# GpSimd's instructions in the order of the kernel's own clock, and a longer margin for ScalarE's steps in the tridiagonal form

## The chip, the cores and the metric

One core of a Trainium2 chip runs the whole program. The time is that of one execution on the device, in microseconds; for the kernel before it is the median of three runs. Engines are named as in the profile: PE is TensorE's matmul, PEld its weight load, DVE is VectorE, ACT is ScalarE, POOL is GpSimd, SP is SyncE.

## What is computed

64 graphs `x` of 256 nodes by 256 features, one matrix `adj` of 256 by 256. Two layers, each `x = x + f(relu(layernorm(x)))`.

```python
# layer 0, w = adj * adj
h = relu(w @ (h @ W1)); h = relu(w @ (h @ W2)); f = w @ (h @ W3)      # 256 -> 512 -> 1024 -> 256 features
# layer 1
deg = adj.sum(0) + adj.sum(1) - diag(adj)
L = rsqrt(deg)[:, None] * (diag(deg) - A) * rsqrt(deg)[None, :]      # A: adj
_, U = eigh(L)
f = U @ (relu((U.T @ h) @ W1 + b1) @ W2 + b2)                        # 256 -> 128 -> 256 features
```

The eigenvectors `U` of one symmetric 256 by 256 matrix are needed before layer 1 can begin; layer 0 doesn't need them.

## The kernel before

Two pieces of work run side by side until the eigenvectors are there.

The **chain** is the eigenvector computation of class `Eigen`: the Laplacian, its tridiagonal form (`tridiagonalize`, 254 steps of Householder's reduction), an iteration on leaves of 16, and four levels of merging. Its steps depend on each other one by one, and most of them run on VectorE.

The **streams** are layer 0 of class `Layers`, over 32 pairs of graphs (`products` and `rows`): large products on TensorE, evictions and norms on ScalarE, and on GpSimd two kinds of work. One is the norm's three operations, `v`, `scale` (a power) and `shift`, named so in the profile. The other is three accumulating transfers a pair, `forms<-forms`, `s<-s` and `s<-forms`.

Class `Pace` interleaves them while the program is written out. It keeps a clock for each engine and the time at which each piece of a tile is written or was read. Every operation of the chain goes through `chain`: its due time is the time at which its operands are ready, plus `LATER` (0.4 us on PE, 0.1 on ACT). Before it is issued, `run` issues operations of the streams, earliest first, as long as `fits` allows: on PE and ACT they have to begin or end before the due time, by the engine of the chain's operation; on every other engine they only have to start before it. `clock` lets GpSimd and VectorE take work back into the past by up to `WINDOW` = 1 us. So `Pace` sets the order in which the instructions are written.

That written order is kept on PE and ACT alone (`manual_schedule` around `eigen.vectors`). On GpSimd, VectorE and SyncE the framework's scheduler orders the instructions by a cost model of its own, the earlier written one first where two are ready.

One step of `tridiagonalize` with `lo < P` (the first 127) goes as follows, by the names of the profile. VectorE makes the new row `xr` (`xn` in the code). ScalarE squares and sums it (`junk<-xr`, the `tail`). GpSimd copies `alpha` (`m<-xr`). VectorE makes `nn`, GpSimd masks the column `xc` (`xc<-xc,lower`), takes the root of `nn` (`s<-nn,half`, `s0` in the code) and the sign of the head (`q<-xr`). VectorE meanwhile updates the matrix `A` and sums `xa` (`r<-A,xr`), then makes `nb` (`m<-q,s`) and `ac`. TensorE turns `ac` and a column of `A` into rows, by transposes of a broadcast (`psB<-ident,ac`, `psA<-ident,A`). GpSimd makes `none` in two operations, VectorE `den`, which reads it, and `z` (`gam`, the reciprocal of `den`). GpSimd makes `gg` and `gu`, VectorE `gc`, and when the rows are back `uau` (`r<-psB,xr`), `gr`, and the next `xr`. The operations on GpSimd are written in this order: `m`, `xc`, `s`, `q`, `none`, `none`, `gg`, `gu`; the transposes are written before `none`.

With `lo >= P` the square, the sign, the mask, `gg` and `gu` are VectorE's, the root is ScalarE's (`s<-nn,guard`), and GpSimd has `m`, a `memset` of half of `xc`, and `none` twice.

After `vectors`, layer 1 runs over all pairs with the rest of layer 0 in between, all engines in written order.

Of the kernel before, what the change touches and what calls it, by code (L numbers as in the profile page):

```python
# [28 lines left out]
P = 128  # L29
# [130 lines left out]
class Pace:  # L160
# [9 lines left out]
    LEAD = 1.5  # L170

    def __init__(self, nc):
        self.slower, self.lead, self.no_haste = self.SLOWER, 0.0, False
        self.now = Proxy(nc, self.chain)
        self.later = Proxy(nc, lambda op: op)
        self.clock = dict.fromkeys(ENGINES.values(), 0.0)
        self.written, self.read, self.streams, self.on = {}, {}, [], True
# [32 lines left out]
    def chain(self, op):  # L210
        if not self.on:
            return op.call(*op.args, **op.kwargs)
        due = self.ready(op) + self.LATER.get(op.engine, 0.0)
        if self.no_haste:
            due = max(due, self.clock[op.engine] + 0.01)
        self.run(due, None if self.no_haste else op.engine)
        return self.issue(op, self.slower)

    def fits(self, op, start, limit, engine):
        if engine is None or op.engine not in ("PE", "ACT"):  # L220
            return start < limit
        if engine == "PE":
            return start < limit + self.HOP * (op.engine == "ACT")
        return start + op.busy + self.lead * (op.engine == "ACT") < limit
# [55 lines left out]
class Eigen:  # L280
# [47 lines left out]
    def row(self, tag):  # L328
        return self.mp.tile([P, N], F32, tag=tag, name=tag)
# [113 lines left out]
    def tridiagonalize(self, a):  # L443
# [14 lines left out]
        def as_row(tag, column, halves):  # L458
            ps = self.psum(tag)
            for h in halves:  # L460
                nc.tensor.transpose(
                    ps[:, h * P : (h + 1) * P],
                    column[:, h : h + 1].to_broadcast([P, P]),
                    ident[:, 0, 0:P],
                )
            return ps
# [9 lines left out]
        def below(xr, lo):  # L476

            rest = slice(lo + 1, N)
            sq, tail, alpha = self.row("junk"), *(t[:, lo - 1 : lo] for t in (tails, alphas))
            if lo < P:  # L480
                nc.scalar.activation(sq[:, rest], xr[:, rest], AF.Square, accum_out=tail)
            else:
                self.stt(sq[:, rest], xr[:, rest], 1.0, xr[:, rest], OP.mult, OP.mult, accum=tail)
            nc.gpsimd.tensor_copy(alpha, xr[:, lo : lo + 1])
            return alpha, tail
# [21 lines left out]
        for k in range(N - 2):  # L507
            lo = k + 1
            r, rest = slice(lo, N), slice(lo + 1, N)
            halves = [0, 1] if lo < P else [1]  # L510
            hs = slice(halves[0], H)
            rc = a[:, :, lo]

            nb = nbs[:, k : k + 1]
            if qn is not None:
                rs, qs = self.col("rs", 1), self.col("qs", 1)
                self.recip(rs, s0)
                self.tt(qs, q, s0, OP.mult)
            xa, junk = self.col("xa"), self.row("r0")
            for h in halves:  # L520
                self.stt(junk[:, r], a[:, h, r], 1.0, xr[:, r], OP.mult, OP.mult, accum=xa[:, h : h + 1])
                if h == halves[0] and qn is not None:
                    self.stt(nb, rs, qn, qs, OP.mult, OP.add)
            if qn is None:
                self.stt(nb, q, 2.0, s0, OP.mult, OP.mult)

            ac, uc = self.col("ac"), us[:, :, k]
            self.stt(ac[:, hs], rc[:, hs], nb, xa[:, hs], OP.mult, OP.add)
            pu, pr = as_row("psB", ac, halves), as_row("psA", rc, halves)

            none = self.col("none", 1)
            nc.gpsimd.tensor_scalar(none, tail, 1e-30, 1e30, OP.is_le, OP.mult)
            nc.gpsimd.tensor_tensor(none, none, nn, OP.add)
            den, gg, gu = (self.col(c, 1) for c in ("den", "gg", "gu"))
            gam = gams[:, k : k + 1]
            u1 = xr[:, lo : lo + 1]
            self.tt(u1, u1, nb, OP.add)
            self.stt(den, alpha, nb, none, OP.mult, OP.add)
            self.recip(gam, den)
            self.stt(uc, ident[:, :, lo], nb, xc, OP.mult, OP.add)  # L540
            aside(lo).tensor_tensor(gg, gam, gam, OP.mult)
            aside(lo).tensor_tensor(gu, gg, u1, OP.mult)
            gc, gr = self.col("gc"), row("gr")
            if halves[0]:
                self.tt(gc[:, hs], ac[:, hs], gam, OP.mult)
            else:
                self.ts(gc, ac, gam, OP.mult)

            uau, c = self.col("uau", 1), self.col("c", 1)
            self.stt(junk[:, r], pu[:, r], 1.0, xr[:, r], OP.mult, OP.mult, accum=uau)  # L550
            self.ts(gr[:, r], pu[:, r], gam, OP.mult)

            xn, xcn, both, f = row("xr"), self.col("xc"), self.row("r1"), self.col("f", 1)
            self.stt(both[:, rest], gr[:, rest], u1, pr[:, rest], OP.mult, OP.subtract)
            self.stt(f, uau, gu, gr[:, lo : lo + 1], OP.mult, OP.subtract)
            self.stt(xn[:, rest], xr[:, rest], f, both[:, rest], OP.mult, OP.subtract)
            more = lo + 1 < N - 1
            if more:
                alpha1, tail1 = below(xn, lo + 1)
            self.stt(c, uau, 0.5, gg, OP.mult, OP.mult)  # L560
            wr, wc = row("wr"), self.col("wc")
            self.stt(wr[:, r], xr[:, r], c, gr[:, r], OP.mult, OP.subtract)
            self.stt(wc[:, hs], uc[:, hs], c, gc[:, hs], OP.mult, OP.subtract)
            if more and halves[0]:
                following = length(xn, lo + 1, tail1)
            if halves[0]:
                nc.gpsimd.memset(xcn[:, 0:1], 0.0)
            self.stt(xcn[:, hs], gc[:, hs], u1, rc[:, hs], OP.mult, OP.subtract)
            self.stt(xcn[:, hs], uc[:, hs], f, xcn[:, hs], OP.mult, OP.subtract)
            aside(lo).tensor_tensor(xcn[:, hs], xcn[:, hs], self.lower[:, hs, lo], OP.mult)  # L570
            if more and not halves[0]:
                following = length(xn, lo + 1, tail1)

            for h in halves:
                self.stt(a[:, h, r], wr[:, r], uc[:, h : h + 1], a[:, h, r], OP.mult, OP.add)
                self.stt(a[:, h, r], xr[:, r], wc[:, h : h + 1], a[:, h, r], OP.mult, OP.add)
            xr, xc = xn, xcn
            if more:
                alpha, tail, (nn, s0, q, qn) = alpha1, tail1, following

        done = slice(0, N - 2)
        e0 = self.row("r1")[:, done]
        self.tt(e0, nbs[:, done], alphas[:, done], OP.add)
# [250 lines left out]
    def all_parts(self, d, bb, es, z, pend, bad):  # L834
# [27 lines left out]
        half = LEAF // 2  # L862
        chain = self.lp.tile([P, 2, half + 1, 3], F32, tag="chain", name="chain")
        nc.vector.memset(chain, 0.0)
        nc.vector.memset(chain[:, :, 0, 0], 1.0)
        invs = self.lp.tile([P, 2, half + 1], F32, tag="invs", name="invs")
# [1465 lines left out]
@with_exitstack  # L2332
def tile_kernel(ctx: ExitStack, tc: tile.TileContext, ap):
    pool = ctx.enter_context(tc.tile_pool(name="shared", bufs=1))
    gt2, u, ut = (pool.tile([P, H, N], F32, name=c) for c in ("gt2", "u", "ut"))
    layers = Layers(tc, ctx, ap, gt2, u, ut)
    layers.open(ctx)
    pace = Pace(tc.nc)
    with ExitStack() as inner:
        eigen = Eigen(tc, inner, ap, gt2, pace)  # L2340

        layers.nc = pace.later
        for op in layers.load(0):
            pace.chain(op)
        layers.nc = pace.now
        eigen.load_matrices(1, 2)
        layers.load_weights()
        eigen.load_rest()

        layers.nc, layers.now = pace.later, pace.now  # L2350
        pace.streams = layers.streams()
        with tc.manual_schedule(engines={mybir.EngineType.PE, mybir.EngineType.Activation}):
            eigen.vectors(u, ut)
            pace.go_on(FLAG_US)
        pace.on = False
        eigen.mend(u, ut)
    pace.on, pace.no_haste, pace.slower = True, True, 1.0
    layers.open1(ctx)
    layers.layer1(pace)
# [33 lines left out]
```

## Time and profile before

| | |
|---|---|
| median of three runs | 2365.49 us (2364.38 to 2368.03) |
| the profiled execution | 2369.36 us, of it the span of instructions 2367.6 us |
| granted TensorE clock, mean | 0.994 |
| busy, share of the span | PE 97%, DVE 85%, ACT 50%, POOL 30% |
| tridiagonal form: last row transposes (`psB<-ident,ac`) at | 1298.4 us |
| the chain's last product (`psC<-bad`) at | 2173.3 us |

In the profile's lists of waits, "POOL m <- DVE xr: 418.0, 224, 7.5" reads: GpSimd was idle for 418.0 us in 224 stretches, the longest 7.5 us, before it wrote `m`, and what ended the idle time was VectorE's writing of `xr`. In the timeline a row has the start, the duration, the engine, the operation with output<-inputs, and in brackets the engine's idle time before it. All chain and stream operations come from one line (L208, the call in `issue`), so they are told apart by their tiles. Matmuls are pipelined: one of 256 columns lasts 377 ns in the profile, and the next starts 216 ns after it.

### The profile page before, as it was taken

Reading aid. Unit: us, or ns where it says so; the run is one execution under the profiler, and the core shown is the slowest. Engines: PE = TensorE matmul, PEld = TensorE weight load, DVE = VectorE, ACT = ScalarE, POOL = GpSimd, SP = SyncE. Lnnn points to the kernel's source line nnn. Section 1 sums busy time; section 2 is a strip of 40 time slices with the busy share of each in tenths; the row PEclk is TensorE's granted clock in tenths of the full one; section 3 lists DMA queues with packets and bytes.
Section 4 is the critical chain, followed back from the end, with each engine's and each line's share of the span. In section 5 each row is a group of like instructions: output and inputs, shape, how many; then the busy total and the mean of one; then the engine's idle time right before and its main releaser. Section 6 shows DMA issues by size and latency. Waiting matters only on the chain. (4 is left out here: it accounts for less than half of the span.)

```text
span 2367.6 us, 40804 instructions
## 1 busy us (share of the span) xinstructions
PE 2290.2 (97%) x10652; PEld 1854.7 (78%) x10652; DVE 2005.0 (85%) x12072; ACT 1183.8 (50%) x2951; POOL 698.7 (30%) x1946
## 2 busy tenths in 40 slices
PE   7999999999999999999999899999999999999999
PEld 4687878787777877787888788777778777887888
DVE  7999999999999999999999899999877687882343
ACT  4455554555555555555555345555554455543322
POOL 3444544445554222222222001111111111111443
PEclk9999999999999999999999999999999999999999
DMA  4022222122222222222222222322322222223675
GB/s 134 23 70 61 65 57 70 51 69 63 59 59 62 72 56 61 69 67 59 72 63 60 58 63 72 72 72 59 72 63 63 59 58 72 54 63 103 217 251 203
DMA packets 91359, 183.26 MB, mean 77 GB/s; under 512 B 8432, under 2 KB 61808, under 8 KB 91120
## 3 DMA queue, kind: packets, MB, share of 16 engines
q0 software_dynamic: 13392, 73.14, 15.6%
q1 hardware_dynamic: 77728, 107.45, 13.4%
q8 instruction: 86, 1.41, 0.2%
q14 instruction: 153, 1.25, 0.2%
HBM read 65.48 MB, written 41.94 MB: 45 GB/s over the span
## 5 line engine op out<-in xcount | busy, mean ns | idle before, releaser
L208 PE MATMUL bank<-forms,L_gnn_W 128*128 128x256 f32 (+2 forms) x2102 | 490.7, 382 | 9.2 <-DVE x L208 6.1
L208 PE MATMUL bank<-L_gnn_W,s 128*128 128x256 f32 x2086 | 476.0, 378 | 4.8 <-ACT s L208 4.7
L208 PEld LDWEIGHTS bank<-forms,L_gnn_W 128*128 128x128 f32 x2102 | 390.6, 191 | 73.3 <-issue 11.7
L208 PEld LDWEIGHTS bank<-L_gnn_W,s 128*128 128x128 f32 x2086 | 391.7, 192 | 57.3 <-ACT s L208 5.7
L208 ACT ACTIVATE s<-bank 128x512 f32<-128x512 f32 (+1 forms) x485 | 278.7, 579 | 174.3 <-PE bank L208 173.3
L208 PE MATMUL bank<-forms,sums 128*128 128x256 f32 (+1 forms) x1512 | 347.0, 377 | 0.0
L208 PEld LDWEIGHTS bank<-forms,sums 128*128 128x128 f32 x1512 | 283.3, 191 | 53.4 <-issue 15.5
L208 PE MATMUL bank<-gt,s 128*128 128x256 f32 (+1 forms) x1036 | 246.3, 377 | 1.1 <-ACT s L208 1.1
L208 PE MATMUL bank<-L_gnn_W,y 128*128 128x512 f32 (+3 forms) x538 | 230.8, 572 | 1.1 <-ACT y L208 1.1
L208 ACT ACTIVATE forms<-bank 128x512 f32<-128x512 f32 x217 | 128.9, 594 | 180.9 <-PE bank L208 180.7
L208 PEld LDWEIGHTS bank<-gt,s 128*128 128x128 f32 x1036 | 188.9, 190 | 24.8 <-ACT s L208 2.6
L208 POOL COPY m<-xr 128x1 f32<-128x1 f32 x254 | 59.9, 236 | 418.1 <-DVE xr L208 418.0
L208 PEld LDWEIGHTS bank<-L_gnn_W,y 128*128 128x128 f32 x538 | 98.7, 190 | 98.2 <-issue 87.3
L208 ACT ACTIVATE junk<-xr 128x254 f32<-128x254 f32 (+63 forms) x127 | 46.0, 362 | 200.5 <-DVE xr L208 200.4
L208 ACT ACTIVATE junk<-x 128x256 f32<-128x256 f32 x256 | 105.8, 413 | 71.9 <-issue 44.0
L208 DVE SCALAR_TENSOR_TENSOR A<-xr,wc,A 128x255 f32<-128x255 f32 (+63 forms) x381 | 139.2, 368 | 0.0
L208 DVE SCALAR_TENSOR_TENSOR A<-wr,q,A 128x255 f32<-128x255 f32 (+63 forms) x381 | 138.0, 365 | 0.0
L208 ACT ACTIVATE junk<-x,nm 128x256 f32<-128x256 f32 x256 | 128.7, 503 | 4.0
L208 PE MATMUL bank<-p,gt 128*128 128x512 f32 (+2 forms) x272 | 122.8, 567 | 0.0
L208 PE MATMUL bank<-gt,h 128*128 128x256 f32 (+1 forms) x520 | 119.1, 379 | 0.1
L208 DVE SCALAR_TENSOR_TENSOR r<-A,xr 128x255 f32<-128x255 f32 (+63 forms) x381 | 117.8, 309 | 0.2
L208 PE MATMUL psB<-ident,ac 128*128 128x128 f32 x381 | 84.7, 277 | 27.2 <-DVE z L208 15.0
(614 smaller groups left out, 4639.5 us busy)
## 6 DMA issues: line engine op xcount, KB each, us to landing
x<-in_x_dram SPq DMA_DIRECT2D x128, 256.0 KB, 3.0
x<-x SPq DMA_DIRECT2D x64, 512.0 KB, 3.5
forms<-forms POOLq DMA_DIRECT2D x31, 768.0 KB, 5.8
s<-s POOLq DMA_DIRECT2D x31, 768.0 KB, 5.9
s<-forms POOLq DMA_DIRECT2D x31, 768.0 KB, 5.8
hw<-hw SPq DMA_DIRECT2D x64, 256.0 KB, 3.1
out_dram<-out SPq DMA_DIRECT2D x64, 256.0 KB, 2.2
L_gnn_W<-in_L_gnn_W_dram SPq DMA_DIRECT2D x1, 2048.0 KB, 11.2
```

Source lines behind the costliest of these rows:

```text
L208: return op.call(*op.args, **op.kwargs)
```

## The change

GpSimd joins PE and ACT: until the eigenvectors are there it runs its instructions in the order in which `Pace` writes them. `fits` gets a rule for it: before a chain operation on GpSimd, a stream's operation on GpSimd has to end, by the clock, before the due time. And a new margin `late` is added to the due time of the chain's operations on ScalarE, 0.5 us in the tridiagonal steps with `lo < P`, 0.2 us in the others, 0 outside of the tridiagonal form.

```diff
@@ Pace
-        self.slower, self.lead, self.no_haste = self.SLOWER, 0.0, False
+        self.slower, self.lead, self.no_haste, self.late = self.SLOWER, 0.0, False, 0.0
...
     def chain(self, op):
...
-        due = self.ready(op) + self.LATER.get(op.engine, 0.0)
+        due = self.ready(op) + self.LATER.get(op.engine, 0.0) + self.late * (op.engine == "ACT")
...
     def fits(self, op, start, limit, engine):
+        if engine == "POOL" == op.engine:
+            return start + op.busy < limit
         if engine is None or op.engine not in ("PE", "ACT"):
             return start < limit
@@ Eigen.tridiagonalize
             hs = slice(halves[0], H)
+            self.pace.late = 0.5 if lo < P else 0.2
...
+        self.pace.late = 0.0
         done = slice(0, N - 2)
@@ tile_kernel
-        with tc.manual_schedule(engines={mybir.EngineType.PE, mybir.EngineType.Activation}):
+        with tc.manual_schedule(engines={mybir.EngineType.PE, mybir.EngineType.Activation, mybir.EngineType.Pool}):
             eigen.vectors(u, ut)
```

## The prediction

> **What bounds the kernel now.** First the page and the table by stage (time, then busy us of PE, PEld, DVE, ACT, POOL). Stage 100 to 740 is the tridiagonal form while `lo < P`, 740 to 1298 the rest of it.
>
> ```profile
> PE 2290.2 (97%) x10652; PEld 1854.7 (78%) x10652; DVE 2005.0 (85%) x12072; ACT 1183.8 (50%) x2951; POOL 698.7 (30%) x1946
> ```
>
> ```profile
> 100.00:740.00 640.00, 625.66 (x3044) 509.11 (x3044) 596.79 (x3025) 342.19 (x904) 317.03 (x972) 1.00 0.26 62
> 740.00:1298.00 558.00, 548.87 (x2626) 444.19 (x2625) 529.88 (x4164) 308.27 (x771) 157.31 (x614) 1.00 0.27 64
> ```
>
> TensorE is busy 98% and VectorE 93 to 95% of both stages. TensorE's work is fixed: layer 0 fills the gaps of the eigenvector chain, layer 1 needs the eigenvectors and comes last, so the end moves by what TensorE's waits change, as long as layer 0 still has work. In the timeline the chain's last product (`psC<-bad`) starts at 2173.3; behind it layer 0 has 46 products of 256 columns (0.216 us from start to start), 8 of 512 (0.429), 24 of 128 (0.11): 9.9 + 3.4 + 2.6 = 16 us. A chain longer by up to 16 us, if TensorE is fed meanwhile, costs nothing; beyond that each us costs one. So I look for TensorE's waits, and ask in the chain of waits who is late. Columns: waiter, releaser, us in total, times, longest. Window 100 to 740, TensorE:
>
> ```profile
> PE psB L208 <- DVE z L208: 13.0, 16, 1.9
> PE psB L208 <- DVE ac L208: 1.2, 2, 1.0
> ```
>
> Window 740 to 1298, TensorE, then VectorE:
>
> ```profile
> PE psB L208 <- DVE xr L208: 9.0, 11, 1.7
> ```
>
> ```profile
> DVE den L208 <- POOL none L208: 3.5, 11, 0.6
> ```
>
> Window 100 to 740, VectorE, then ScalarE:
>
> ```profile
> DVE r L208 <- PE psB L208: 15.1, 45, 1.0
> DVE m L208 <- POOL s L208: 9.4, 27, 1.1
> ```
>
> ```profile
> ACT junk L208 <- DVE xr L208: 177.1, 106, 5.1
> ```
>
> TensorE waits 14.2 us in the first form and 9.2 in the second, always before the row transposes of `ac`, that is, for the chain. ScalarE sits idle 177.1 us before the chain's square (`junk<-xr`), 1.6 us in each of 111 steps, with layer operations queued behind it. VectorE waits 9.4 us for the root `s` on GpSimd. One step with each. ScalarE and TensorE around 424.46:
>
> ```profile
> 421.69 0.36 ACT L208 ACTIVATE junk<-xr 128x189 f32<-128x189 f32 x1 [0.79 <-DVE xr L208]
> ...
> 422.05 1.07 ACT L208 ACTIVATE h<-x,shift,scale 128x256 f32<-128x256 f32 x2
> 423.03 1.56 ACT L208 ACTIVATE s<-s 128x1024 f32<-128x1024 f32 x2
> ```
>
> ```profile
> 424.46 0.40 PE L208 MATMUL psB<-ident,ac 128*128 128x128 f32 x2 [1.60 <-DVE z L208]
> ```
>
> TensorE ran dry: its next products need the rectified `s`, and that stands on ScalarE behind a square for which ScalarE idled 0.79 us. GpSimd around 491:
>
> ```profile
> 488.32 0.40 POOL L208 TENSOR_SCALAR v<-v 128x4 f32<-128x4 f32 x1 [1.42 <-ACT junk L208]
> 488.80 1.05 POOL L208 TENSOR_TENSOR scale<-v,rsqrt 128x4 f32<-128x4 f32 x1
> 489.93 0.20 POOL L208 TENSOR_TENSOR shift<-nm,scale 128x4 f32<-128x4 f32 x1
> 490.07 0.31 POOL L208 COPY m<-xr 128x1 f32<-128x1 f32 x1
> 490.36 0.32 POOL L208 TENSOR_SCALAR q<-xr 128x1 f32<-128x1 f32 x1
> 490.65 0.32 POOL L208 TENSOR_TENSOR xc<-xc,lower 128x2 f32<-128x2 f32 x1
> 491.06 0.24 POOL L208 TENSOR_SCALAR none<-m 128x1 f32<-128x1 f32 x1
> 491.38 0.56 POOL L208 TENSOR_TENSOR s<-nn,half 128x1 f32<-128x1 f32 x1
> ```
>
> `nn` was written at 489.71, yet `s` begins at 491.38: behind a layer's norm and four small chain operations. VectorE loses 1.05 us and TensorE's next transposes 1.12.
>
> **The margin on ScalarE.** No instruction is added. The due time of the square grows by 0.5 us (of the second form's `Sqrt` by 0.2), so layer work on ScalarE that ends up to that much later, and products on TensorE, go ahead. Of the first form's 14.2 us about 6 follow a stall on `s` (the eight largest VectorE stalls, 0.45 to 1.05 us, sum to 6.3); 8 are dry waits as at 424. A rectification of 1.05 us or an eviction of 0.58 that has 0.79 us of idle time needs 0 to 0.3 us more, which 0.5 gives; I take five eighths: -5. In the second form 0.2 us admits an eviction, not a rectification: a third of 9.2, -3. At worst neither fits: 0. The price: a square delayed by 0.2 to 0.5 us holds `nn`, which VectorE runs right behind it. If a third of 111 steps is late by 0.3, the chain is 11 us longer, under the 16 us that TensorE can fill, so I cost it at nothing; without that cover it is +11.
>
> **GpSimd's order, the chain's own operations.** Emission order is m, xc, s, q, none, none, where the profile has m, q, xc, none, s, none. `s` no longer waits for `q` and `none`. Counted from the end of `xr`, medians of the timeline's steps: `nn` ends at 0.78 us, `s` runs from 1.28 to 1.96, VectorE takes `nb` at 2.07 and `den` at 2.46. In the new order `s` runs 0.85 to 1.5, `q` to 1.8, the two `none` (some 0.3 each) to 2.4: `nb`'s operands come 0.15 us earlier, `den`'s at the last moment. Nineteen of the 27 stalls are below 0.2 us, 3.1 us in all; they go, and a third of the eight large ones (2.1): -5. Bounds: -9.4 (all) and +6 (`den` late by 0.05 us in each of 111 steps).
>
> **GpSimd's order, the layers' operations.** They are emitted at the first chain step whose due time lies behind their start, and the transposes of `ac` are emitted before `none`. So a layer operation that can start before `ac` is ready now stands ahead of `none`, which `den` needs. Counting starts in the timeline, 16 of the first form's 46 groups (28 transfers, 18 norms) begin in the first 2.5 us after `xr`, and 25 of the second's 44 in the first 2.3 us. A transfer holds GpSimd 0.97 us (the row below), a norm 1.03 + 0.23 + 0.25 = 1.5.
>
> ```profile
> L208 POOL DMA_DIRECT2D s<-s x9 | 8.8, 978 | 4.6 <-ACT s L208 4.0 <-issue 0.6
> ```
>
> First form: `none` ends near 1.8 + 0.97 + 0.55 = 3.4 instead of 2.4, `den` wanted at 2.46. But VectorE can't pass the row products anyway until the transposes are back at 3.7 (median), and only `den`, `z` and `gc`, half a us, stand between: a loss of 0 to 0.25, 16 x 0.12 = 2 us. Second form: rows back at 2.8, `den` wanted at 1.9, `none` done near 3.1: 0.3 each, 25 x 0.3 = 7.5, of which the slack of TensorE takes half (VectorE waits for `psB` there too). Sum +5.75, from 0 to 16 x 0.9 + 25 x 1.2 = +44, the whole delay of `den`. After 1298 GpSimd is 10 to 13% busy and its chain operations are few: 0, from -2 to +3.
>
> The Trainium skill speaks to both parts. "DMA: Bandwidth & Descriptors", in Anatomy of one DMA, calls descriptor generation small; by it a transfer ahead of `none` would be free and the +5.75 about +2. The row has 978 ns, and the row decides. "TensorE: Matmul & The Clock Gate", in its table of specifications, gives GpSimd a strict queue of 8: a rule against this change, since what waits at the head holds the chain behind it; the rows at 488 to 491 agree (1.67 us from `nn` to `s`), but they hold for the old order as well, so by the rule nothing is added.
>
> Sum: -5 - 3 - 5 + 5.75 = -7.25. The profiled execution took 2369.36 us, so 2362.1; it lies 3.9 us above the median of the runs, 2365.49. Against the median: 2358.
>
> **The rivals.** (1) Slower: `none` behind the layers' operations becomes the bound. For it: 41 groups stand in that stretch, and transfers whose producer on ScalarE is late would hold `none` longer still. Against: the round trip over TensorE hides most of it in the first form. It decides once a group delays `den` past the return of the rows, 1.2 us in the first form, 0.9 in the second. At half the full price, 22 us, and the lengthened square eating the 16 us of cover, less 8 of gains: +14, 2380. (2) The rule for GpSimd doesn't bite: before the square, layer operations on GpSimd are only asked to start before the limit, and that limit now lies 0.6 us behind `xr`; they still go ahead of m. The stalls of 1.05 us stay, `none` costs its 5.75, and the margin's 8 remain: -2, 2363. (3) The chain and TensorE are balanced, and waits saved at one step come back as VectorE's waits for `psB` (15.1 us now); with the delayed squares: 2366.
>
> **How the numbers follow.** About 0.2% (4.7 us) is what a measurement can tell from no change. Forecast 0.46, rival 1 0.32, rival 2 0.12, rival 3 0.10. Of the forecast nine tenths lie beyond -4.7 us, and of rivals 2 and 3 a third: faster 0.48; slower is rival 1 and a little of 3: 0.35; the rest 0.17. Best end: all of the 9.4 and 12 of the 17 dry us, with the full 5.75 of cost: -16, 2349. Rival 1 spreads to +17 before only its tail is left: 2382. The forecast's own range is 2351 to 2362.
>
> **What would show it.** Right: the waits of `psB` in the two windows fall from 14.2 and 9.2 to some 8 and 6, the wait of `m` (`nb`) for `s` from 9.4 to under 6, ScalarE's idle time before the square from 177.1 to some 135, `den`'s wait for `none` rises to about 10. Wrong: that wait goes over 20 us, TensorE waits more before `psB`, or the last product of the chain comes after 2189 and TensorE idles until layer 1 begins.

## The result: slower by 1.2%

The changed kernel takes 2393.77 us (median of four, 2393.29 to 2395.31) against 2366.35 us for the kernel before on the same chip (2364.38 to 2368.03). The ratio is 1.0117, 95% interval 1.0100 to 1.0135. The forecast was 2358 us; the time lies above its range too, and on the other side of no change.

The profile after, in the order in which the prediction read that of before. First the page's list of engines and the table by stage:

```profile
PE 2295.4 (96%) x10662; PEld 1853.0 (77%) x10662; DVE 2018.3 (84%) x12072; ACT 1186.1 (50%) x2951; POOL 690.8 (29%) x1946
```

```profile
100.00:740.00 640.00, 604.80 (x2922) 488.53 (x2921) 578.20 (x2885) 332.70 (x876) 297.86 (x930) 1.00 0.25 60
740.00:1298.00 558.00, 542.57 (x2596) 439.44 (x2595) 519.41 (x3984) 296.76 (x732) 152.28 (x608) 1.00 0.26 63
```

The work is the same (VectorE has its 12072 instructions again), but in the same 640 us TensorE got through 2922 products instead of 3044, and VectorE through 2885 instructions instead of 3025: both the layers and the chain have slowed down. The chain of waits in the window 100 to 740 (waiter, releaser, us in total, times, longest):

```profile
PE psB L208 <- DVE z L208: 29.8, 27, 2.6
PE psB L208 <- DVE ac L208: 3.4, 6, 0.8
DVE den L208 <- POOL none L208: 18.5, 22, 1.8
DVE r L208 <- PE psB L208: 12.9, 30, 1.3
DVE m L208 <- POOL q L208: 7.5, 14, 0.9
ACT junk L208 <- DVE xr L208: 141.6, 84, 4.9
```

And in the window 740 to 1298:

```profile
PE psB L208 <- DVE xr L208: 13.6, 24, 1.6
DVE den L208 <- POOL none L208: 10.9, 18, 1.5
```

TensorE's waits before the transposes of `ac` more than doubled in the first form (14.2 to 33.2 us), and VectorE's `den` now waits for `none` 29.4 us in all, where it waited 3.7. The profile names `z` or `xr` as the releaser, instructions that stand behind `ac` on VectorE; what the transposes read is `ac`. In the second form TensorE's wait of 13.6 us was 8.2 before in the same window; the prediction's 9.0 is the answer for a window that ends at 1299. ScalarE's idle time before the square did fall, nearly to the forecast's 135: the margin does what it says. One step of the changed kernel shows the new wait, in the timeline of GpSimd, VectorE and TensorE:

```profile
146.56 0.37 POOL L208 TENSOR_SCALAR q<-xr 128x1 f32<-128x1 f32 x1
147.07 0.22 POOL L208 TENSOR_SCALAR v<-v 128x4 f32<-128x4 f32 x1
147.37 1.20 POOL L208 TENSOR_TENSOR scale<-v,rsqrt 128x4 f32<-128x4 f32 x1
148.64 0.23 POOL L208 TENSOR_SCALAR none<-m 128x1 f32<-128x1 f32 x1
148.96 0.19 POOL L208 TENSOR_TENSOR none<-none,nn 128x1 f32<-128x1 f32 x1
```

```profile
149.19 0.22 DVE L208 SCALAR_TENSOR_TENSOR den<-m,none 128x1 f32<-128x1 f32 x1 [1.50 <-POOL none L208]
149.32 0.21 DVE L208 SCALAR_TENSOR_TENSOR ac<-A,m,xa 128x2 f32<-128x2 f32 x1
```

```profile
149.68 0.40 PE L208 MATMUL psB<-ident,ac 128*128 128x128 f32 x2 [2.45 <-DVE z L208]
```

A layer's norm stands between `q` and `none`. `den` waits 1.50 us for it, and `ac`, which doesn't read `none`, stands behind `den` in VectorE's queue. So the transposes come late as well, and TensorE is dry for 2.45 us.

This form of the loss is the rarer one. From 100 us on, 25 steps of the first form have a layer's operation ahead of `none`; in only six of them `ac` stands behind `den`. In the other 19 the scheduler has put `ac` ahead, as here (`ac` starts at 290.16), and the transposes run on time, while `den` and what follows it are late:

```profile
290.58 0.38 PE L208 MATMUL psB<-ident,ac 128*128 128x128 f32 x2
```

```profile
291.90 0.22 DVE L208 SCALAR_TENSOR_TENSOR den<-m,none 128x1 f32<-128x1 f32 x1 [1.45 <-POOL none L208]
292.81 0.37 DVE L208 SCALAR_TENSOR_TENSOR r<-psB,xr 128x214 f32<-128x214 f32 x1
```

The transposes of `ac` end at 290.96, and their rows are read at 292.81. TensorE loses nothing in this step; the next `xr`, and with it the next transposes, come late.

To compare kernels whose chains run at different speeds, I take TensorE's time apart. After each product's start I allow what the trace gives as its issue interval (0.064 us for 1 column, 0.11 for 128, 0.216 for 256, 0.322 for 384, 0.429 for 512; twice that where the granted clock is 0.5). What the next start is later than that, above 15 ns, is a gap. The extra of the doubled intervals is the loss to the low clock. The intervals themselves sum to 2255 us in every kernel. All of it is from the one profiled execution of each; medians and ratios are from the timed runs, each ratio against the kernel before in the same job (2366.35, 2368.52, 2365.74 and 2366.12 us). The windows are the same for all, though the tridiagonal form ends later in the slower kernels (its last transposes start at 1336.7 us after, 1298.4 before; the steps with `lo < P` end at 787 and 763).

| kernel | median us | ratio to before (95%) | gaps 100 to 740 | gaps 740 to 1298 | other gaps | low clock |
|---|---|---|---|---|---|---|
| before | | 1 | 19.9 | 13.9 | 57.4 | 11.6 |
| after | 2393.77 | 1.0117 (1.0100 to 1.0135) | 44.8 | 22.2 | 51.6 | 7.8 |
| pool_only | 2395.78 | 1.0114 (1.0097 to 1.0130) | 41.2 | 28.7 | 53.0 | 9.2 |
| margin_only | 2374.82 | 1.0028 (1.0016 to 1.0039) | 26.3 | 14.5 | 59.1 | 6.2 |
| none_early | 2363.24 | 0.9981 (0.9972 to 0.9991) | 26.4 | 13.7 | 51.6 | 4.7 |
| none_and_root | 2357.74 | 0.9952 (0.9936 to 0.9969) | 22.5 | 13.9 | 51.3 | 3.1 |
| ac_first | 2384.15 | 1.0073 (1.0057 to 1.0088) | 37.9 | 22.1 | 55.5 | 3.1 |
| best_m00 | 2364.45 | 0.9995 (0.9986 to 1.0004) | 25.6 | 16.3 | 51.2 | 3.6 |
| best_m50 | 2357.53 | 0.9970 (0.9960 to 0.9980) | 21.7 | 18.8 | 49.2 | 0 |
| best_m02 | 2365.41 | 1.0002 (0.9993 to 1.0011) | 25.8 | 18.1 | 49.2 | 4.5 |
| early_first | 2370.54 | 1.0019 (1.0010 to 1.0028) | 26.9 | 22.6 | 49.4 | 4.3 |
| early_second | 2385.07 | 1.0076 (1.0064 to 1.0088) | 45.1 | 13.5 | 51.8 | 8.1 |
| margin_first | 2377.06 | 1.0052 (1.0039 to 1.0065) | 26.0 | 14.4 | 57.4 | 12.9 |
| margin_second | 2368.95 | 1.0007 (0.9998 to 1.0016) | 20.4 | 14.3 | 57.0 | 11.3 |

From before to after: +24.9 in the first form's window, +8.3 in the second's, -5.8 elsewhere, -3.8 of low clock: +23.6, and the span grew by 23.9 (2367.6 to 2391.5).

### The profile page after: what moved, and what is told of

Read it like the earlier page. It is cut to its first block, busy times and chain, and to the rows that moved or that the text cites. A ratio compares the mean times of both kernels' runs of the same rounds, so it can differ in the third digit from the quotient of the medians.

```text
span 2391.5 us, 40806 instructions
## 1 busy us (share of the span) xinstructions
PE 2295.4 (96%) x10662; PEld 1853.0 (77%) x10662; DVE 2018.3 (84%) x12072; ACT 1186.1 (50%) x2951; POOL 690.8 (29%) x1946
## 3 DMA queue, kind: packets, MB, share of 16 engines
q1 hardware_dynamic: 77728, 107.45, 13.5%
## 5 line engine op out<-in xcount | busy, mean ns | idle before, releaser
L208 PE MATMUL bank<-forms,sums 128*128 128x256 f32 x1518 | 346.7, 375 | 0.0
L208 PE MATMUL bank<-L_gnn_W,y 128*128 128x512 f32 (+2 forms) x532 | 231.0, 577 | 1.1 <-ACT y L208 1.1
L208 PEld LDWEIGHTS psB<-ident,ac 128*128 128x128 f32 x381 | 45.7, 136 | 109.3 <-issue 49.7
L208 PE MATMUL bank<-p,gt 128*128 128x512 f32 (+3 forms) x270 | 125.0, 579 | 0.0
```

## The experiments

The theory after the result: layers' operations ahead of `none` make the loss. The rivals: GpSimd's order of the chain's own operations, and the margin.

**none_early.** The changed kernel with the two operations of `none` written in `length`, right behind `s` and `q` (behind `qn` in the second form), before any layer's operation of that step can come between.

```diff
 def length(xr, lo, tail):
...
-                return nn, s0, q, None
+                return nn, s0, q, None, masked(nn, tail)      # masked: the two operations of none
...
-            return nn, s0, q, qn
+            return nn, s0, q, qn, masked(nn, tail)
```

> The change, with the two none operations written right behind the root and the sign, so that no layer operation can stand between q and none; the chain's own order m, xc, s, q, none, none stays. Theory: most of the loss is gone, 2360 to 2375 us, den's wait for none under 8 us. Rival A: still 2385 to 2395. Rival B: still 2385 to 2395.

Measured: 0.9981. The whole loss is gone: 1.36 points of the ratio, 32 us, against the changed kernel. 18.4 us of gaps vanish in the first form and 8.5 in the second, and `den`'s wait for `none` is 1.9 and 0.6 us in the two windows. That is the theory, shown by taking its cause away with everything else of the change in place. It came out at 2363.2 us, inside the theory's range and far from both rivals'.

**pool_only and margin_only.** The change without the margin (`late` kept at 0), and the kernel before with the margin alone.

```diff
-            self.pace.late = 0.5 if lo < P else 0.2
+            self.pace.late = 0.0
```

> The change without its margin on ScalarE (late is 0 throughout). Theory (layers' operations stand ahead of none on GpSimd, den waits for them): as slow as the changed kernel, 2385 to 2400 us, and den's wait for none stays near 29 us over the tridiagonal form. Rival A (GpSimd's own chain order, s and q ahead of none, is the cost): 2385 to 2400 as well. Rival B (the margin delays the square and with it the chain): 2370 or less.

> The kernel before with the margin on ScalarE alone; GpSimd's order is the scheduler's again and has no rule of its own. Theory: 2356 to 2367 us, since the margin lets layer work go ahead and none is not held. Rival A: the same. Rival B: 2385 or more.

Measured: 1.0114 and 1.0028. GpSimd's order carries the loss. The margin adds nothing to it, and by itself it costs 6 us instead of bringing 8: its 2374.8 us lie above the theory's range and below that of rival B, so neither had it.

**none_and_root.** As none_early, but with `lo < P` the operations are written as m, xc, q, none, s, none. That is the order in which the kernel before ran them, but for `xc` and `q`, which stood the other way round there.

```diff
-                self.power(s0, nn, 0.5)
                 nc.gpsimd.tensor_scalar(q, x1, 0.0, 0.5, OP.is_ge, OP.subtract)
-                return nn, s0, q, None, masked(nn, tail)
+                none = self.col("none", 1)
+                nc.gpsimd.tensor_scalar(none, tail, 1e-30, 1e30, OP.is_le, OP.mult)
+                self.power(s0, nn, 0.5)
+                nc.gpsimd.tensor_tensor(none, none, nn, OP.add)
+                return nn, s0, q, None, none
```

> As none_early, and in the form with lo below 128 the chain's own order is m, xc, q, none, s, none, so that q and the first none no longer stand behind the root. Theory: within 6 us of none_early, 2358 to 2372. Rival A: only here the loss goes, 2368 or less, 15 us or more below none_early. Rival B: still 2385 to 2395.

Measured: 0.9952, so the old order is the better one, by 3.9 us of gaps in the first form. VectorE's and TensorE's waits in the window 100 to 740:

```profile
PE psB L208 <- DVE z L208: 14.1, 17, 2.7
DVE m L208 <- POOL s L208: 12.6, 35, 1.1
```

Here `nb` waits more for the root than it waits for GpSimd in none_early, which has `s` in front (5.4 us, there for `q`), and still the step is shorter. Means over the first form's steps, counted from the end of `xr`: with `s` in front (none_early) `nb` starts at 2.12 us, `den` at 2.72, `ac` at 2.83; with the old order at 2.20, 2.61, 2.73. What `nb` gains, `den` loses behind `none` (done at 2.66 instead of 2.30), and `ac` follows `den`.

**ac_first.** The changed kernel with `den` held behind `ac` in VectorE's queue.

```diff
-            self.stt(ac[:, hs], rc[:, hs], nb, xa[:, hs], OP.mult, OP.add)
+            made = self.stt(ac[:, hs], rc[:, hs], nb, xa[:, hs], OP.mult, OP.add)
...
-            self.stt(den, alpha, nb, none, OP.mult, OP.add)
+            with self.tc.issue_after(made.ins):
+                self.stt(den, alpha, nb, none, OP.mult, OP.add)
```

> The change, with den kept behind ac on VectorE (an ordering edge, no wait): GpSimd's order is the changed one. Theory (den waits for none at the head of VectorE's queue and holds ac, and so the row transposes on TensorE): half of the loss or more is gone, 2380 us or less, TensorE's waits before psB in the first form fall from 33.9 to under 22 us. Rival (z and gr need den anyway, the order of den and ac is idle): 2388 or more.

Measured: 1.0073, 2384.2 us, between the two. In the window 100 to 740:

```profile
PE psB L208 <- DVE xr L208: 23.2, 27, 2.6
DVE den L208 <- POOL none L208: 15.5, 14, 1.7
```

With 3.7 us for `ac` TensorE waits 26.9 us before the transposes, where the theory wanted under 22. The gaps of the first form fall by 6.9 us of the 18.4 that none_early takes away, those of the second form not at all (22.1): there `ac` stood ahead of `den` in 125 of 126 steps of the changed kernel already, so the edge has nothing to move. In the first form the fall sits in the six steps with `ac` behind `den`, where the gaps of the step go from 10.8 to 3.3 us. So `ac` behind `den` is a good third of the first form's gaps. It is less of the steps' time: against the same steps of none_early the 25 are 19.0 us longer in the changed kernel, 6.3 of it in those six and 12.7 in the 19 where `ac` went ahead, and ac_first takes back 3.8 of the 19.0. The rest is `den` itself: `z`, `gr` and the next `xr` are later, and the next transposes with them.

**early_first and early_second.** none_early in the steps of one form alone: in the other `none` is written where the change has it. In the changed kernel 25 steps of the first form and 22 of the second have a layer's operation ahead of `none`; they last 6.573 and 4.853 us, the others 5.789 and 4.269. That would be 25 x 0.784 + 22 x 0.584 = 19.6 + 12.8 = 32.4 us.

```diff
-            return nn, s0, q, qn, masked(nn, tail)            # early_first: lo >= P as in the change
+            return nn, s0, q, qn, None
...
+            if none is None:
+                none = masked(nn, tail)
             self.stt(den, alpha, nb, none, OP.mult, OP.add)
```

> The two operations of none are written behind s and q in the steps with lo < P alone; in the others they stay where the change has them. Theory, from the steps of the changed kernel that have a layer's operation ahead of none (25 of 6.573 us against 5.789 us for the others, 22 of 4.853 against 4.269 in the second form: 19.6 and 12.8 us): three fifths of the loss come back, some -18 us against the changed kernel, about 2375, ratio to before 1.004. Rival, the prediction's proportion (2 us in the first form, 3.75 in the second): a third comes back, -10 us, about 2383, ratio 1.007.

> The two operations of none are written behind nn in the steps with lo >= P alone. Theory (12.8 of 32.4 us): -12 us against the changed kernel, about 2381, ratio to before 1.0065. Rival (the prediction's proportion, two thirds in the second form): -20 us, about 2374, ratio 1.003.

Measured: 1.0019 and 1.0076; against the changed kernel 0.98 and 0.41 points, 23 and 10 us. The theory's proportion holds, with more than forecast in the first form (23 us, not 18), and the rival's falls. The waits of early_first show the mended form and the other beside it, `den` in the window 100 to 740 and then in 740 to 1298:

```profile
DVE den L208 <- POOL none L208: 2.1, 12, 0.2
```

```profile
DVE den L208 <- POOL none L208: 11.6, 18, 1.5
```

**best_m00, best_m50, best_m02.** none_and_root with the margin at 0 and 0, 0.5 and 0, 0 and 0.2 us (first form, second form).

> none_and_root without any margin on ScalarE. Theory (the margin only delays the chain, as margin_only showed by 6 us): 2350 to 2355 us. Rival (the margin pays once GpSimd's order is right, by the forecast's 8 us): 2362 to 2368.

> none_and_root with the margin of 0.5 us in the form with lo below 128 alone. Theory: the whole price of the margin is here, since there the square is the head of the step: 2356 to 2360, as none_and_root. Rival: 2357 or above with the gain lying here, best_m02 then is 2362 or more.

> none_and_root with the margin of 0.2 us in the second form alone. Theory: within 2 us of best_m00, 2350 to 2356. Rival: 2360 or more.

Measured: 0.9995, 0.9970, 1.0002. The theory that the margin only delays falls. GpSimd's written order without a margin leaves the time as it was; all of the gain comes with the first form's 0.5, and an effect of the 0.2 can't be told from none.

**margin_first and margin_second.** The kernel before with one of the two margins.

> Before with the margin of 0.5 us in the steps with lo < P alone. Theory: the loss of the whole margin (+6.5 us) comes from the 0.5, because under the scheduler's own order of GpSimd the later square holds s behind a layer's operations: about 2372 to 2373, ratio 1.0028, and VectorE's wait of m for s stays near 13.7 us. Rival: the 0.5 pays here too, as it does with GpSimd's order written (-7 us), and the loss is the second form's: 2360, ratio 0.997.

> Before with the margin of 0.2 us in the steps with lo >= P alone. Theory: as with GpSimd's order written, where it moved nothing: 2366, ratio 1.000. Rival: the second form carries the loss: 2372 or more, ratio 1.003 or more.

Measured: 1.0052 and 1.0007. The first form's margin is what costs, +6.1 us of gaps there. The 11 us of margin_first are more than the 6 us of margin_only, which has both margins and the same gaps in that form (26.3 and 26.0); the two profiles differ in the low clock, 12.9 us against 6.2. Its waits in 100 to 740:

```profile
PE psB L208 <- DVE z L208: 18.1, 21, 2.4
DVE m L208 <- POOL s L208: 13.2, 32, 1.5
ACT junk L208 <- DVE xr L208: 133.0, 76, 4.9
```

ScalarE idles 44 us less before the square, as planned, and the chain pays for it: `nn` starts 0.083 us later in the mean step, `nb` 0.075, the rows are read 0.092 later, and the step takes 5.910 us instead of 5.823, which makes the chain 0.087 x 122 steps = 10.6 us longer. Between best_m00 and best_m50 the same margin moves `nn` by 0.047 us, but `nb` by only 0.014, and the step gets shorter, 5.840 to 5.828: there the later square seems to be taken up by the root, which stands behind other work on GpSimd. Why it doesn't do so under the scheduler's order isn't settled by these runs.

## Why the prediction was wrong, step by step

**The layers' operations ahead of `none`: +5.75 forecast, 27 to 32 us measured.** This is the step that failed. Its mechanism was right, and its count nearly (41 groups forecast, 47 steps found). The price of one was not: 0.12 us in the first form and 0.15 in the second, where the steps show 0.78 and 0.58. Three things are behind it.

First, the wait was longer than drawn. In the 25 steps `none` ends at 3.81 us in the median, not 3.4, and `den` starts at 4.03. The forecast counted the time that a layer's operation runs, 0.97 or 1.5 us. But in a written order GpSimd also waits at that operation for its operand, with `none` behind it. Idle time of GpSimd in front of such operations that ScalarE ended comes to 5.3 us in the first form's steps and 10.8 us in the second's, for example here, with GpSimd free from 840.88 on and `none` next in line:

```profile
842.25 0.97 POOL L208 DMA_DIRECT2D s<-s  x1 [1.37 <-ACT s L208]
```

Rival 1 had named this, as transfers whose producer on ScalarE is late; the sum had no term for it.

Second, the cover was too short. The forecast rested on the sentence that "VectorE can't pass the row products anyway until the transposes are back" at 3.7 us. In the 19 steps with `ac` ahead the rows are indeed read from 3.73 us in the median, but `den` starts at 3.97 and `z` is done at 4.39, with `gr` and the next `xr` after it. In ten of these steps VectorE's own order has `den` even behind the row product; what that order costs by itself wasn't tried.

Third, in six steps the cover moved with the wait. The transposes need `ac`, and there `ac` stands behind `den` on VectorE: the wait that was to be hidden holds what hides it (6.9 us of gaps by ac_first).

In the second form the forecast let the slack of TensorE take half, and the steps show no such slack.

**GpSimd's own order: -5 forecast, about +4 in the first form's gaps.** The prediction had named the way this could fail, `den`'s operands "at the last moment", and priced it at a bound of +6. In none_early, without any layer's operation in between, `none` ends at 2.56 us in the median of the steps from 100 to 740, not at 2.4, and `den` starts 0.10 us later than in none_and_root.

**The margin: -5 and -3 forecast; nothing in the changed kernel, +11 us alone in the first form, +6 with both, and between -0.5 and +3.8 us in the second (margin_second's interval).** The dry waits were real, and ScalarE did use its idle time. But the delay of the chain was costed "at nothing", under 16 us of layer 0 that TensorE could still fill in. That cover hardly exists. In the changed kernel the chain's last product (`psC<-bad`) comes at 2198.4 instead of 2173.3, 25 us later, and the layer-0 work left behind it went only from 16.0 to 10.8 us: 5 us were filled, 20 were waited. TensorE runs in the written order, so where the chain is later than planned it stands before the transposes with other work queued behind them. The same holds for the kernel before with the first form's margin alone (margin_first): last product at 2182.4, 9 us later, and the same 16.0 us left.

**After 1298: 0 forecast, from -2 to +3.** The gaps there fell by 2.4 us, just past that range. Two things were not in the forecast at all: the gaps of the first 100 us fell by 3.4, and the loss to the low clock by 3.8. Together they hide nearly 10 us of the loss. And the chain behind the tridiagonal form got shorter: from the last row transposes to its last product it takes 861.7 us after and 874.9 before. It takes 853 to 866 us in all ten kernels with GpSimd's written order and 872 to 875 in the four without; why wasn't tried.

**The rivals.** Rival 1 (slower, 2380) had the cause, but at a price of 22 us where 27 to 32 were measured, and at a third of the chance. The signs of "wrong" came: `den` waits 29.4 us for `none` (bound 20), TensorE waits more before `psB`, and the chain ends after 2189, though TensorE's gaps between its end and the end of the program grew by only 2 us. Rival 2, that the rule doesn't bite, is out: of the first form's stalls of `nb` above 0.3 us, three of eight had a norm ahead of the root before, with up to 1.05 us, and two of eleven have a layer's operation there after, with 0.32 us each. The wait as such went from `s` to `q`, which now stands behind `s`, and from 9.4 to 7.5 us. Rival 3's balance isn't what is seen: VectorE's waits for `psB` went from 15.1 to 12.9 us in the first form and from 6.2 to 10.3 in the second, 2 us more in all.

**A version that beats both kernels.** none_and_root (0.9952) and best_m50 (0.9970) do. But not by what the change was forecast to mend: in the tridiagonal form their gaps (36.4 and 40.5 us) are no smaller than those of the kernel before (33.8). They gain in the other gaps (-6 and -8) and in the low clock (-8.5 and -11.6), which the last section takes up. An earlier end of the chain isn't the gain by itself: best_m00 has the chain's last product at 2151.6, 22 us before that of the kernel before and ahead of both of these (2157.0 and 2155.9), leaves 29 us of layer 0 behind it, and takes as long as the kernel before.

## What to carry to other kernels

Before a wait is called hidden, price the whole of it: in a written order the operation ahead holds the queue while it waits for its own operand, not only while it runs. Then follow what hides the wait back to its own operands and through every queue they pass: in six steps here the cover stood behind the waiting instruction, and in the others it ended before the wait did. Work that is left over at the end is cover for a delay only if the order of instructions lets an engine reach it; with a written order, an unplanned delay is waited out. And an order made by a clock has to place an operation where its operands are ready, not where the program happens to need its result: two lines moved up in the code gave back 32 us.

## What was not expected of the hardware

The granted clock took part in every comparison. The kernel before has it at 0.993 to 0.997 in its timed runs, best_m50 at 0.997 to 1.0; runs of best_m50 took 2356.1 us (median of four) at 1.0 and 2362.3 at 0.997. The profiled executions show where: stretches of 3.4, 6.8 or once 10.2 us at a clock of 0.5. In the 14 profiles there are 45 of them before the last 8 us, and each begins in a gap of TensorE of at least 2.15 us or within 3.6 us of its end. Of the gaps over 2 us after the first 50 us, 51 have no such stretch; the longest of these is 3.21 us, and every longer one has it. Two windows of the kernel before (the column before the DMA share is the clock), and the two waits that belong to them, from the chain of waits of TensorE in 1340 to 2090 and in 2090 to 2225:

```profile
1740.00:1780.00 40.00, 36.24 (x150) 28.00 (x149) 22.34 (x157) 24.05 (x59) 8.03 (x13) 0.91 0.32 81
2150.00:2170.00 20.00, 15.18 (x69) 12.83 (x68) 8.29 (x20) 6.74 (x13) 2.28 (x3) 0.83 0.33 65
```

```profile
PE bank L208 <- ACT s L208: 4.7, 2, 3.8
PE psA L208 <- DVE m L208: 4.8, 1, 4.8
```

So a wait of 4.8 us cost up to 7.9: the wait, and the work lost in a stretch of 6.8 us at half the clock, which begins 0.6 us before its end (half of 6.2 us). best_m50 has no gap above 2.94 us past its start, and no such stretch before its end; best_m00 still has one of 7.53 us, before layer 1's first product, and loses 3.6 us in its low stretches. This is where much of the gain of the best versions sits. The profiles of the kernel before and of best_m50 overstate it: their spans differ by 13.3 us, the medians of the timed runs by 8.2, with a clock of 0.995 and 0.999 in the median run. Why GpSimd's written order breaks up the long waits of the merging levels is open; and the link between gap and clock is read from the traces and wasn't tried by itself.

The Trainium skill, "TensorE: Matmul & The Clock Gate", in its part on the HAM clock gate, has a rule for it: a window of about 3.4 us without enough work halves the clock until a busy window has passed. The lengths of 3.4 and 6.8 us agree with it; the gaps behind which it is seen here begin at 2.15 us, shorter than a whole window.
